# Odd column tiles of a deformable convolution: copied by VectorE and ScalarE in place of DMA transfers, with the pixels of a tile laid column by column

## The chip, the cores and the metric

The kernel runs on one core of one Trainium2 chip, all in 32-bit floats. The metric is the device time of one execution in microseconds (us). The program shown takes 1498.91 us, the median of three runs (1492.4 to 1503.4). The profiled execution is one run of its own, at 1483.92 us.

## The reference, cut to what matters

The input is `x`, 8 images of 128 channels and 64 x 64 pixels. Layer 0 is a group norm and a modulated deformable 3 x 3 convolution, followed by a batch norm over all images and a ReLU. Layer 1 is a group norm and a mixture of four 3 x 3 convolutions and a shared one. The change touches only the deformable convolution:

```python
om = conv(x, off_w) + off_b                      # 27 maps: 9 taps of (dy, dx, mask)
off, mask = om[:, :18], sigmoid(om[:, 18:])
py = dy + row - 1 + ky ; px = dx + column - 1 + kx
val = sum over the four corners of (py, px): weight(corner) * x[corner]   # bilinear
val = val * mask
out = einsum('bckhw,ock->bohw', val, w)
...
x = x + layer0(group_norm(x))
x = x + layer1(group_norm(x))
```

## The kernel before, in words

**Bilinear sampling as a matrix product.** Offsets are taken to be smaller than two pixels (`REACH` 2; if not, a general path runs instead, which these inputs do not take). The samples of a tile of 4 rows by 4 columns (`T` 4) then lie inside a patch of 8 by 8 pixels (`Q` 8, `HALF` 64 pixels). A *band* is two such rows of tiles, `h` = 0 and 1, that is 8 image rows; an image has 8 bands (`NB`), all images 64. A band has 15 column tiles (`NCOL`), which step by 4 columns while a patch is 8 wide, so neighbouring patches overlap by half. The 8 even tiles (`EVEN`) cover the row without overlap; each of the 7 odd tiles consists of the right half of one even patch and the left half of the next.

For every tile a matrix `xts` of 128 partitions by 128 channels holds the pixels: the partition is the pixel of the patch (64 for `h` = 0, then 64 for `h` = 1). Before the change the partition order is `h`, patch row, patch column. The sampling weights are the product of a weight by column, `x_wts`, and one by row, `y_wts`; both have the pixel on the partition.

**The steps of a band `g`:**

- `pick(g)` (L763): VectorE copies the even patches out of the normalised image `pads` into `picked`, two copies of 512 elements.
- `pixels(g)` (L779): TensorE transposes four tiles at a time (L799) into one PSUM tile, ScalarE copies it into `xts` (L802). This is done twice for the even tiles. Only the very first band also makes its odd tiles in this way, from `picked_odd` (L786).
- `share(g)` (L807): fills the odd tiles. For each of the 8 patch columns a transfer takes 16 partitions (one column, all rows, stride 8) of seven even tiles and writes the same partitions of the seven odd tiles. It is issued on SyncE's queue (SP), for one band on GpSimd's (POOL).
- `load_x(g)` (L730) and `load_y(g, k)` (L713): transfers from the tables `x_table` and `y_table` in DRAM into `x_wts` and `y_wts`. A call of `load_y` serves one of the 8 image rows: 5 patch rows (`NR`) by 8 patch columns, 40 partitions, each getting the 9 x 64 floats (`YSTEP`) of its row distance. The parts of `y_wts` out of reach stay zero. In the loop they are issued on POOL, at `q` = 2 and 3.
- `spread(g)` (L746): turns column distances into weights, an Abs on ScalarE with the bias `columns` (L755, L758) and a clip on VectorE (L761).
- `weights(n)` (L822): VectorE multiplies the two weights for one of five groups of three tiles (L837) into `s`, of which there are four buffers; it runs three groups ahead.
- `sample(n)` (L843): TensorE multiplies pixels and weights (L853): 60 matmuls a band, four for each tile, tile after tile from 0 to 14. ScalarE copies the result into `samples` (L863). The PSUM tile `pq` has three buffers.
- `close(g)` (L874) and `conv(g)` (L890): the 3 x 3 convolution of the samples, 9 taps (L902), an eviction by ScalarE (L910) and a store to `ydram` on SP (L912).

**Tables.** `tables(b)` (L308) computes, for an image two ahead, the group norm (means by L317, applied by ScalarE in L342 and VectorE in L346), the offset convolution (combined rows L370, L420, L422; matmuls L389, L455), and from the offsets the tables: gathers through DRAM (`rowwise`, `colwise`, issued on SP in L522, L529, L553, L567), row and column distances on VectorE (L612 to L627), tent functions on ScalarE (L637, L641), masks on VectorE (L674), and the stores `store_x` (L592) and `store_y` (L664). The image itself comes in four quarters by `load_quarter` (L280, SP); `statistics` (L302) reads them.

**What sets the order.** The stage is under a manual schedule: each engine and each queue runs its instructions in the order in which the program issues them. The loop is written by hand (L991): for each band, first the five groups (weights, sample, row-weight loads at `q` 2 and 3), then the taps of the *previous* band's convolution, and between the taps (`part` 0 to 8) everything else: `pixels(g + 2)` at parts 0 and 1, `load_x(g + 3)` at 2, `spread(g + 2)` at 1, 3, 5 and 7, `share(g + 2)` at 3, `pick(g + 3)` and a quarter at 4, and three steps of `tables` after each part (`tick`). `xts` has two buffers, `y_wts` two, `x_wts` three.

Of the kernel before, what the change touches and what calls it, by code (L numbers as in the profile page):

```python
# [11 lines left out]
ALU = mybir.AluOpType  # L12
# [4 lines left out]
P = 128  # L17
H = W = 64
# [21 lines left out]
REACH = 2  # L40
NR = 2 * REACH + 1
T = 4
Q = T + 2 * REACH
HALF = Q * Q
NCOL = 15
NROW = H // T
# [3 lines left out]
EVEN = (NCOL + 1) // 2  # L50
# [5 lines left out]
YSTEP = TAPS * W  # L56
GROW = NR * YSTEP
BLOCK = "block"
OFF_AT = 16
XROW = (NCOL + 1) * T * XSTEP  # L60
# [5 lines left out]
def deform_moe_conv(  # L66
# [18 lines left out]
    nc = tc.nc  # L85
# [10 lines left out]
        out=gsel, in_=gsel, compare_op=ALU.is_ge, fill=0.0, base=0,  # L96
# [3 lines left out]
        out=gsel, in_=gsel, compare_op=ALU.is_ge, fill=0.0, base=3,  # L100
# [49 lines left out]
    def padded(pool, name):  # L150
# [10 lines left out]

    tables_y, tables_x = (
        [dram.tile([n], F32, name=f"tab{a}{i}") for i in range(2)]
        for a, n in (("y", H * GROW), ("x", NROW * XROW))
    )
    y_table, x_table = ([t[b % 2] for b in range(B)] for t in (tables_y, tables_x))

# [12 lines left out]
    def dense():  # L180

        with ExitStack() as st:
# [44 lines left out]

            place_i = a1.tile([P, 3], I32, name="place_i")  # L230
            place = a1.tile([P, 3], F32, name="place")
            beside = a1.tile([P, 1], F32, name="beside")
            for i, base, mask in ((0, T - REACH, T - 1), (1, 0, Q - 1), (2, T, Q - 1)):
                one = place_i[:, i : i + 1]
                nc.gpsimd.iota(one, pattern=[[0, 1]], base=base, channel_multiplier=1)
                nc.vector.tensor_single_scalar(one, one, mask, op=ALU.bitwise_and)
# [5 lines left out]
                    pattern=[[0, 1]], channel_multiplier=sign,  # L242
                )
            nc.vector.tensor_tensor(place[:, 0:1], place[:, 0:1], beside, ALU.add)
            nc.vector.tensor_scalar(place[:, 1:3], place[:, 1:3], -1.0, None, ALU.mult)
            in_tile, columns = place[W:P, 0:1], (place[:, 1:2], place[:, 2:3])

            combos = [a1.tile([P, H // 2, W], F32, name=f"combo{i}") for i in range(2)]
# [19 lines left out]
            xts, ss, late = {}, {}, []  # L268
# [39 lines left out]
            def tables(b):  # L308
# [265 lines left out]
                for k, *where in by_column:  # L574
                    turned_in(nc.sync if b or k == 0 else nc.gpsimd, k, *where)
                if b == 0:
                    share(1, nc.sync)
                yield from pause((50, 9)[b] if b < 2 else 35)

                def moved(side, t, *dims):  # L580
# [81 lines left out]
                def store_y(i, n, rows=slice(0, H)):  # L662

                    nc.sync.dma_start(  # L664
                        out=bass.AP(
                            tensor=y_table[b].tensor,
                            offset=y_table[b].offset + rows.start * GROW + i * YSTEP,
                            ap=[[GROW, rows.stop - rows.start], [1, n * YSTEP]],
                        ),
                        in_=work[rows, i : i + n].rearrange("p i n -> p (i n)"),  # L670
                    )

                def masked(i):
# [27 lines left out]
                for i in (3, 0, 4, 1, 2):  # L701
                    masked(i)
                    store_y(i, 1, soon)
                for k in range(2 * T):
                    load_y(0, k, (nc.sync, nc.gpsimd, nc.scalar, nc.gpsimd)[k % 4])
                for _ in statistics(1):
                    pass
                for tiles in ((NCOL, NCOL + 1), (0, 3), (3, 9), (9, NCOL)):
# [2 lines left out]
                store_x(6, NROW, nc.sync)  # L711
                store_y(0, NR, slice(4 * T, H))

            def load_y(g, k, engine):

                if g >= len(bands):
                    return
                b, j = bands[g]
                h, r = divmod(k, T)
                at = HALF * h + r * Q  # L720
                engine.dma_start(  # L721
                    out=y_wts[g % 2][at : at + NR * Q, r].rearrange("p a b c -> p (a b c)"),
                    in_=bass.AP(
                        tensor=y_table[b].tensor,
                        offset=y_table[b].offset + (2 * T * j + k) * GROW,
                        ap=[[YSTEP, NR], [0, Q], [1, YSTEP]],
                    ),
                )

# [33 lines left out]
            def pick(g):  # L763

                if g >= len(bands):
                    return
                b, j = bands[g]
                for h in range(2):
                    one = pads[b % 2][:, 2 * T * j + T * h : 2 * T * j + T * h + 1, 0:1]
                    nc.vector.tensor_copy(  # L770
                        picked[g % 2][:, :, h],
                        bass.AP(
                            tensor=one.tensor, offset=one.offset,
                            ap=[list(one.ap[0]), [Q, EVEN], [W, Q], [1, Q]],
                        ),
                    )


            def pixels(g, turn_odd=False):  # L779

                if g >= len(bands):
                    return
                xts[g] = a2.tile([P, NCOL, P], F32, name="xt")
                if turn_odd:
                    for side in range(2):
                        nc.vector.tensor_copy(  # L786
                            picked_odd[:, :, :, :, T * side : T * side + T].rearrange(
                                "p c h y x -> p c (h y) x"
                            ),
                            picked[g % 2][  # L790
                                :, 1 - side : EVEN - side, :, :, T * side : T * side + T
                            ].rearrange("p c h y x -> p c (h y) x"),
                        )
                for c0 in range(0, NCOL if turn_odd else EVEN, 4):
                    n = min(4, NCOL - c0)
                    pt = ps_c.tile([P, 4, P], F32, name="pt", tag="pc")
                    for c in range(c0, c0 + n):
                        one = picked[g % 2][:, c] if c < EVEN else picked_odd[:, c - EVEN]
                        nc.tensor.transpose(  # L799
                            pt[:, c - c0], one.rearrange("p h y x -> p (h y x)"), ident  # L800
                        )
                    nc.scalar.copy(xts[g][:, c0 : c0 + n], pt[:, 0:n])  # L802
                    yield

            def share(g, engine):  # L807

                if g >= len(bands):
                    return  # L810
                for x0 in range(T):
                    for side in range(2):
                        rows = slice(x0 + T * side, P, Q)
                        engine.dma_start(  # L814
                            out=xts[g][rows, EVEN:].rearrange("p c n -> p (c n)"),
                            in_=xts[g][rows, 1 - side : EVEN - side].rearrange("p c n -> p (c n)"),
                        )

            def width(q):
                return GT * T + 2 * (q in (0, NGR - 1))  # L820
# [170 lines left out]
            for g in range(len(bands) + 1):  # L991
# [24 lines left out]
                for done, _ in enumerate(taps):  # L1016
                    part, odd = divmod(done, twice)
                    if odd == 0 and part in PIXELS:
                        next(turned, None)
                    if odd == 0 and part == 2:  # L1020
                        load_x(g + 3, nc.gpsimd)
                    if odd == 0 and part in SPREAD:
                        step, half = divmod(SPREAD.index(part), 2)
                        if step:
                            spread(g + 2, HALVES[half], ())
                        else:
                            spread(g + 2, sides_=(half,), clip=False)
                    if odd == 0 and part == 3:
                        share(g + 2, nc.gpsimd if g == 3 else nc.sync)
                    if odd == 0 and j == NB - 3 and part in (0, 1, 2, 4):  # L1030
                        for _ in range(2):
                            next(means_of, None)
                    if odd == 0 and j == NB - 3 and part == 7 and b + 2 < B:
                        for _ in made:
                            pass
                        asked, made = True, tables(b + 2)
                        next(made)
                    if odd == 0 and part in BLOCKS and asked:
                        asked = False
                        tick()  # L1040
                    for _ in range(3 + (g < NB) if twice == 1 else 1 + done % 2):
                        tick()
                    if odd == 0 and part == 4:
                        pick(g + 3)
                        if 2 <= j < 5:
                            load_quarter(b + 2, j - 1)
                    if odd == 0 and part == 8 and j == 1:
                        load_quarter(b + 2, 0)
                for _ in turned:
                    pass  # L1050
                if g == 0:
                    share(2, nc.sync)
                    load_x(3, nc.gpsimd)
                    pick(3)
                    spread(1)
                    for n in range(AHEAD):
                        weights(NGR + n)
                    spread(2)
# [605 lines left out]
```

## Time and profile before

| | us |
|---|---|
| median of three runs | 1498.91 |
| the profiled execution | 1483.92 |
| its span, first to last instruction | 1482.1 |
| the sampling stage, from the first L853 to the last | 71 to 1090 |

| busy in the profiled execution | us | of the span |
|---|---|---|
| TensorE (PE) | 1312.5 | 89% |
| VectorE (DVE) | 961.2 | 65% |
| ScalarE (ACT) | 786.3 | 53% |
| GpSimd (POOL) | 450.7 | 30% |

| instructions that the change touches | count | mean or median each |
|---|---|---|
| `xt<-xt` on SP, L814 | 496 transfers of 56 KB | 587 ns of issue |
| `xt<-xt` on POOL, L814 | 8 transfers of 56 KB | 489 ns of issue, 8.4 us to landing |
| `ywts<-taby` on POOL, L721 | 508 transfers of 90 KB | 611 ns of issue, 5.5 us to landing |
| `picked<-pad`, DVE, L770 | 128 copies of 128x512 | 420 ns |
| `xt<-pt`, ACT, L802 | 130 copies | 584 ns |

Busy shares are averages over the whole span. The row of slices cuts the span in 40 equal parts of 37 us; the sampling stage lies in slices 2 to 29, layer 1 follows. `PEclk` is the TensorE clock granted, in tenths of full speed. In a timeline each line has the start, the length, the engine, the line of the code, the operation, its output and inputs and a count; the bracket gives the idle time before it and the instruction or landing that ended it. `SPq` is SyncE's queue issuing transfers.

### The profile page before, as it was taken

Reading aid. Unit: us, or ns where it says so; the run is one execution under the profiler, and the core shown is the slowest. Engines: PE = TensorE matmul, PEld = TensorE weight load, DVE = VectorE, ACT = ScalarE, POOL = GpSimd, SP = SyncE. Lnnn points to the kernel's source line nnn. Section 1 sums busy time; section 2 is a strip of 40 time slices with the busy share of each in tenths; the row PEclk is TensorE's granted clock in tenths of the full one; section 3 lists DMA queues with packets and bytes.
Section 4 is the critical chain, followed back from the end, with each engine's and each line's share of the span. In section 5 each row is a group of like instructions: output and inputs, shape, how many; then the busy total and the mean of one; then the engine's idle time right before and its main releaser. Section 6 shows DMA issues by size and latency. Waiting matters only on the chain.

```text
span 1482.1 us, 22076 instructions
## 1 busy us (share of the span) xinstructions
PE 1312.5 (89%) x7561; PEld 750.7 (51%) x7561; DVE 961.2 (65%) x1987; ACT 786.3 (53%) x1057; POOL 450.7 (30%) x759
## 2 busy tenths in 40 slices
PE   4169789899998998997999899979985999999997
PEld 1144456565655655664565565656542444444443
DVE  5546666577667755855775685634418887878872
ACT  2355755666675675676567667856624323232320
POOL 6343333343333343343333334344302101011000
PEclk9579979999999998999999899999996999999999
DMA  4496775997798798788869898998908444565411
GB/s 145 116 198 167 168 178 139 199 230 195 183 217 217 170 208 210 190 190 208 194 172 209 208 209 197 206 216 204 219 23 250 133 124 136 147 170 157 113 48 55
DMA packets 136416, 256.27 MB, mean 173 GB/s; under 512 B 81426, under 2 KB 84654, under 8 KB 127606
## 3 DMA queue, kind: packets, MB, share of 16 engines
q0 software_dynamic: 55600, 137.91, 42.9%
q1 hardware_dynamic: 80532, 116.45, 28.1%
q8 instruction: 62, 1.02, 0.3%
q14 instruction: 60, 0.49, 0.1%
q10 hardware_dynamic: 162, 0.41, 0.1%
HBM read 180.23 MB, written 45.35 MB: 152 GB/s over the span
## 4 chain that ended last, share of the span: by engine, by line
PE 44%; DMA 26%; DVE 12%; issue 8%; SPq 5%; ACT 3%; POOL 1%; DVEq 0%; POOLq 0%; ACTq 0%
PE py L902 15%; PE pc L1576 13%; PE pq L853 10%; DMA xt<-xt 10%; DMA pad<-in_x_dram 5%; DMA combo<-rowwise 4%; PE pc L455 2%; DMA yd<-y 2%; PE pt L799 2%; SPq L814 2%; DMA ywts<-taby 2%; SPq L567 2%; DVE combo L422 2%; DMA x<-in_x_dram 1%; DVE s L837 1%
## 5 line engine op out<-in xcount | busy, mean ns | idle before, releaser
L902 PE MATMUL py<-samples,dw_sb 128*128 128x512 f32 (+3 forms) x1296 | 555.9, 564 | 9.5 <-ACT y L910 7.6
L721 POOL DMA_DIRECT2D ywts<-taby x508 | 298.5, 611 | 485.2 <-DVE s L837 381.5
L853 PE MATMUL pq<-s,xt 64*128 64x144 f32 (+1 forms) x3840 | 301.4, 313 | 79.1 <-DVE s L837 48.0
L853 PEld LDWEIGHTS pq<-s,xt 64*128 64x128 f32 x3840 | 272.7, 201 | 124.5 <-issue 45.3
L902 PEld LDWEIGHTS py<-samples,dw_sb 128*128 128x128 f32 x1296 | 229.7, 191 | 208.6 <-issue 178.2
L863 ACT COPY samples<-pq 128x864 f32<-128x864 f32 (+1 forms) x320 | 284.5, 975 | 84.8 <-PE pq L853 84.3
L837 DVE TENSOR_TENSOR s<-xwts,ywts 128x72 f32<-128x72 f32 (+1 forms) x447 | 200.6, 500 | 89.9 <-PE pq L853 76.8
L761 DVE TENSOR_SCALAR xwts<-xwts 128x1152 f32<-128x1152 f32 (+2 forms) x128 | 93.1, 757 | 176.6 <-ACT xwts L755 168.5
L1576 PE MATMUL pc<-v,u 128*128 128x512 f32 x384 | 174.2, 600 | 6.3 <-DVE v L1483 6.3
L1576 PE MATMUL pc<-v,wmix 128*128 128x512 f32 x384 | 174.4, 599 | 0.0
L755 ACT ACTIVATE xwts<-xwts,place 128x1152 f32<-128x1152 f32 (+3 forms) x132 | 152.9, 1162 | 31.3 <-DMA xwts<-tabx 31.3
L1554 ACT ACTIVATE t<-pc,bmix 128x512 f32<-128x512 f32 x32 | 22.0, 687 | 187.5 <-PE pc L1576 98.8
L1576 PEld LDWEIGHTS pc<-v,u 128*128 128x128 f32 x384 | 72.0, 191 | 92.8 <-issue 83.9
L1576 PEld LDWEIGHTS pc<-v,wmix 128*128 128x128 f32 x384 | 72.4, 190 | 91.4 <-issue 89.5
L910 ACT ACTIVATE y<-py,db_sb 128x512 f32<-128x512 f32 (+3 forms) x72 | 45.7, 635 | 130.4 <-PE py L902 88.7
L802 ACT COPY xt<-pt 128x512 f32<-128x512 f32 (+1 forms) x130 | 75.9, 584 | 59.8 <-PE pt L799 55.8
L736 POOL DMA_DIRECT2D xwts<-tabx x128 | 76.3, 608 | 96.1 <-DMA tabx<-combo 33.6
L799 PEld LDWEIGHTS pt<-ident,picked 128*128 128x128 f32 x512 | 59.5, 141 | 75.4 <-ACT xt L802 39.7
L799 PE MATMUL pt<-ident,picked 128*128 128x128 f32 x512 | 79.8, 279 | 5.0 <-ACT xt L802 3.0
L674 DVE TENSOR_TENSOR work<-work,combo 64x576 f32<-64x576 f32 x40 | 29.6, 747 | 46.3 <-ACT work L641 46.3
L982 DVE BATCH_NORM_STATS2 ystats<-y 128x6 f32<-128x512 f32 (+3 forms) x72 | 44.6, 627 | 20.1 <-ACT y L910 20.1
L302 DVE BATCH_NORM_STATS2 stats<-pad 128x6 f32<-128x512 f32 x64 | 39.7, 826 | 14.7 <-DMA pad<-in_x_dram 14.7
(204 smaller groups left out, 1090.6 us busy)
## 6 DMA issues: line engine op xcount, KB each, us to landing
xwts<-tabx POOLq DMA_DIRECT2D x128, 576.0 KB, 8.5
ywts<-taby POOLq DMA_DIRECT2D x508, 90.0 KB, 5.5
xt<-xt SPq DMA_DIRECT2D x496, 56.0 KB
pad<-in_x_dram SPq DMA_DIRECT2D x36, 512.0 KB
out_dram<-yo SPq DMA_DIRECT2D x32, 512.0 KB
yd<-y SPq DMA_DIRECT2D x48, 256.0 KB
pad<-yd SPq DMA_DIRECT2D x16, 512.0 KB
x<-yd SPq DMA_DIRECT2D x16, 512.0 KB
```

The source lines that it names most:

```text
L721: engine.dma_start(out=y_wts[g % 2][at : at + NR * Q, r].rearrange("p a b c -> p (a b c)"), in_=bass.AP(tensor=y_table[b].tensor, offset=y ...
L736: engine.dma_start(out=x_wts[g % 3][HALF * h : HALF * h + HALF], in_=bass.AP(tensor=x_table[b].tensor, offset=x_table[b].offset + (2 * j + ...
L755: nc.scalar.activation(some, some, AF.Abs, bias=columns[side])
L761: nc.vector.tensor_scalar(some, some, -1.0, 0.0, ALU.add, ALU.min)
L799: nc.tensor.transpose(pt[:, c - c0], one.rearrange("p h y x -> p (h y x)"), ident)
L802: nc.scalar.copy(xts[g][:, c0 : c0 + n], pt[:, 0:n])
L837: engine.tensor_tensor(s[:, :, 3 * at : 3 * (at + k)].rearrange("p m (c x) -> p m c x", x=3), by_x[:, :, c : c + k], by_y[:, :, w : w + k] ...
L853: nc.tensor.matmul(by_m[:, h, :, at : at + k], lhsT=xts[g][rows, c // 2 + EVEN * (c % 2)], rhs=s[rows, :, at : at + k], start=True, stop=True,
L863: nc.scalar.copy(bass.AP(tensor=one.tensor, offset=one.offset + first, ap=[list(one.ap[0]), [M * PLANE, 2], [PLANE, M], [WB + 1, 3], [1, w ...
L902: nc.tensor.matmul(py, lhsT=dw_sb[:, 3 * (2 - yy) + 2 - xx], rhs=samples[g % 2][:, m : m + 3 * n - 2 : 3, xx, 1 : W + 1], start=(i == 0), ...
L910: nc.scalar.activation(y, py, AF.Identity, bias=db_sb)
L1576: nc.tensor.matmul(pc, lhsT=us[j][:, kx], rhs=vs[g][:, rows, kx : kx + W], start=(kx == 0), stop=(kx == 2),)
```

## The change

All odd tiles after the first band's are now made by compute engines. The order of the pixels on the partitions becomes `h`, patch column, patch row. The four left and right halves of the patches are then four blocks of 32 partitions that lie together, so `share` becomes four copies of 32 partitions and 896 floats: the two left halves by VectorE, the two right halves by ScalarE, issued at parts 2, 3 (VectorE), 4 and 6 (ScalarE). The new order needs other things: `pick` and the transposes read the patch column first; the biases `columns` are built from another part of the partition number; and the row weights of one patch row now sit 8 partitions apart, so `load_y` serves one of 8 patch rows of both halves (16 partitions) with up to four image rows in one run. For that the y table in DRAM is laid out in runs by patch row: `store_y` writes each row distance `T * YSTEP` floats apart, and the table is longer at its end. At the start, `load_y` of the first band is called once for each half, 16 calls in place of 8.

```diff
-        for a, n in (("y", H * GROW), ("x", NROW * XROW))
+        for a, n in (("y", H * GROW + 4 * NR * YSTEP), ("x", NROW * XROW))
...
-            for i, base, mask in ((0, T - REACH, T - 1), (1, 0, Q - 1), (2, T, Q - 1)):
+            for i, base, mask in ((0, T - REACH, T - 1), (1, 0, HALF - Q), (2, HALF // 2, HALF - Q)):
...
-            nc.vector.tensor_scalar(place[:, 1:3], place[:, 1:3], -1.0, None, ALU.mult)
+            nc.vector.tensor_scalar(place[:, 1:3], place[:, 1:3], -1.0 / Q, None, ALU.mult)
...
-                    share(1, nc.sync)
+                    for piece in range(4):
+                        share(1, piece, MOVES[piece])
...
-                            offset=y_table[b].offset + rows.start * GROW + i * YSTEP,
-                            ap=[[GROW, rows.stop - rows.start], [1, n * YSTEP]],
+                            offset=y_table[b].offset + rows.start * GROW + i * T * YSTEP,
+                            ap=[[GROW, rows.stop - rows.start], [T * YSTEP, n], [1, YSTEP]],
                         ),
-                        in_=work[rows, i : i + n].rearrange("p i n -> p (i n)"),
+                        in_=work[rows, i : i + n],
...
-                for k in range(2 * T):
-                    load_y(0, k, (nc.sync, nc.gpsimd, nc.scalar, nc.gpsimd)[k % 4])
+                for k in range(Q):
+                    for h in range(2):
+                        load_y(0, k, (nc.sync, nc.gpsimd, nc.scalar, nc.gpsimd)[k % 4], (h,))
...
-            def load_y(g, k, engine):
+            def load_y(g, k, engine, halves=(0, 1)):
...
-                h, r = divmod(k, T)
-                at = HALF * h + r * Q
+                first, last = max(0, k - 2 * REACH), min(T - 1, k)
+                n, h = len(halves), halves[0]
                 engine.dma_start(
-                    out=y_wts[g % 2][at : at + NR * Q, r].rearrange("p a b c -> p (a b c)"),
+                    out=y_wts[g % 2][
+                        HALF * h + k : HALF * (h + n) : Q, first : last + 1
+                    ].rearrange("p r a b c -> p (r a b c)"),
                     in_=bass.AP(
                         tensor=y_table[b].tensor,
-                        offset=y_table[b].offset + (2 * T * j + k) * GROW,
-                        ap=[[YSTEP, NR], [0, Q], [1, YSTEP]],
+                        offset=y_table[b].offset
+                        + (2 * j + h) * T * GROW + (T * k + first) * YSTEP,
+                        ap=[[T * GROW, n]] * (n > 1)
+                        + [[0, Q], [1, (last + 1 - first) * YSTEP]],
                     ),
                 )
...
-                            ap=[list(one.ap[0]), [Q, EVEN], [W, Q], [1, Q]],
+                            ap=[list(one.ap[0]), [Q, EVEN], [1, Q], [W, Q]],
...
-            def share(g, engine):
+            def share(g, piece, move):
...
-                for x0 in range(T):
-                    for side in range(2):
-                        rows = slice(x0 + T * side, P, Q)
-                        engine.dma_start(
-                            out=xts[g][rows, EVEN:].rearrange("p c n -> p (c n)"),
-                            in_=xts[g][rows, 1 - side : EVEN - side].rearrange("p c n -> p (c n)"),
-                        )
+                side = piece % 2
+                rows = slice(HALF // 2 * piece, HALF // 2 * (piece + 1))
+                move(
+                    out=xts[g][rows, EVEN:].rearrange("p c n -> p (c n)"),
+                    in_=xts[g][rows, 1 - side : EVEN - side].rearrange("p c n -> p (c n)"),
+                )
+
+            MOVES = (nc.vector.tensor_copy, nc.scalar.copy) * 2
...
-                    if odd == 0 and part == 3:
-                        share(g + 2, nc.gpsimd if g == 3 else nc.sync)
+                    if odd == 0 and part in (2, 3, 4, 6):
+                        piece = {2: 0, 3: 2, 4: 1, 6: 3}[part]
+                        share(g + 2, piece, MOVES[piece])
...
-                    share(2, nc.sync)
+                    for piece in range(4):
+                        share(2, piece, MOVES[piece])
```

Left out are the same change of order, row and column exchanged, in the copies and the transpose of `pixels`.

More of the change, by code (lines that the diff above doesn't have):

```diff
@@ L786, in pixels @@
                         nc.vector.tensor_copy(
-                            picked_odd[:, :, :, :, T * side : T * side + T].rearrange(
-                                "p c h y x -> p c (h y) x"
+                            picked_odd[:, :, :, T * side : T * side + T].rearrange(
+                                "p c h x y -> p c h (x y)"
                             ),
                             picked[g % 2][
-                                :, 1 - side : EVEN - side, :, :, T * side : T * side + T
-                            ].rearrange("p c h y x -> p c (h y) x"),
+                                :, 1 - side : EVEN - side, :, T * side : T * side + T
+                            ].rearrange("p c h x y -> p c h (x y)"),
                         )
@@ L799, in pixels @@
                         nc.tensor.transpose(
-                            pt[:, c - c0], one.rearrange("p h y x -> p (h y x)"), ident
+                            pt[:, c - c0], one.rearrange("p h x y -> p (h x y)"), ident
                         )
```

## The prediction

> **What bounds the kernel now.** I read the page first: busy shares, the row of slices, the chain.
>
> ```profile
> span 1482.1 us, 22076 instructions
> PE 1312.5 (89%) x7561; PEld 750.7 (51%) x7561; DVE 961.2 (65%) x1987; ACT 786.3 (53%) x1057; POOL 450.7 (30%) x759
> ...
> PE   4169789899998998997999899979985999999997
> ...
> PEclk9579979999999998999999899999996999999999
> DMA  4496775997798798788869898998908444565411
> ...
> PE 44%; DMA 26%; DVE 12%; issue 8%; SPq 5%; ACT 3%; POOL 1%; DVEq 0%; POOLq 0%; ACTq 0%
> PE py L902 15%; PE pc L1576 13%; PE pq L853 10%; DMA xt<-xt 10%; DMA pad<-in_x_dram 5%; DMA combo<-rowwise 4%; PE pc L455 2%; DMA yd<-y 2%; PE pt L799 2%; SPq L814 2%; DMA ywts<-taby 2%; SPq L567 2%; DVE combo L422 2%; DMA x<-in_x_dram 1%; DVE s L837 1%
> ```
>
> In slices 2 to 29, the sampling stage that the change touches, TensorE is full except once per batch, where a 7 stands and PEclk dips; DMA is at 7 to 9. The copies `xt<-xt` are 10% of the chain. So the second view is the timeline around one dip.
>
> ```profile
> 676.42 8.23 SPq L814 DMA_DIRECT2D xt<-xt  x8
> ...
> 683.62 0.64 PE L853 MATMUL pq<-s,xt 64*128 64x216 f32 x4
> ...
> 685.84 8.84 SPq L814 DMA_DIRECT2D xt<-xt  x8
> ...
> 691.52 6.04 PE L853 MATMUL pq<-s,xt 64*128 64x144 f32 x56 [7.25 <-DMA yd<-y]
> ...
> 695.04 2.55 SPq L592 DMA_DIRECT2D tabx<-combo  x6
> ...
> 697.70 0.41 SPq L280 DMA_DIRECT2D pad<-in_x_dram  x1
> ...
> 707.25 0.35 PE L317 MATMUL pm<-mv,gsel 128*128 128x1 f32 x2 [1.60 <-DVE mv L305]
> ```
>
> Four of the 60 sampling matmuls are tile 0; the fifth is tile 1, the first odd tile, and there TensorE stands 7.25 us, whatever landing the releaser names. The eight copies hold SyncE for 8 to 9 us of a band that takes 13.2 us undisturbed. The image quarter (L280, 697.70) queues behind them; its statistics then stop TensorE again. The 56 matmuls take 6.04 us where they take 3.83 us undisturbed: the clock has dropped.
>
> Over the stage, waits at the first odd tile are 2.27, 5.73, 0.86, 1.58, 0.73, 2.12, 0.89, 7.25, 6.43 and 0.49: **28 us**. Waits of L317 are 8.25, 5.22, 4.39, 1.60 and 0.40: **20 us**. Sampling and mean matmuls stretched after those waits lose about **17 us** (1.67, 2.06, 1.66, 2.21 and 2.80 in the 56-matmul groups, the rest after L317).
>
> The third view is ScalarE, in a plain band and then in one that builds tables.
>
> ```profile
> 652.07 1.12 ACT L755 ACTIVATE xwts<-xwts,place 128x1008 f32<-128x1008 f32 x1
> 656.31 0.69 ACT L910 ACTIVATE y<-py,db_sb 128x512 f32<-128x512 f32 x1 [3.12 <-issue]
> ```
>
> ```profile
> 430.02 0.69 ACT L641 ACTIVATE work<-work 64x576 f32<-64x576 f32 x1
> 430.62 0.66 ACT L910 ACTIVATE y<-py,db_sb 128x512 f32<-128x512 f32 x1
> ```
>
> The plain band leaves 3.1 us ahead of the eviction, the table band nothing. VectorE is the same in the band of the combos (columns: window and length, then busy us of PE, PEld, DVE, ACT, POOL, clock, DMA share, GB/s):
>
> ```profile
> 600.00:613.00 13.00, 12.90 (x104) 6.71 (x102) 12.83 (x16) 6.66 (x10) 3.05 (x6) 1.00 0.73 191
> ```
>
> [...] copies of 512 and 768 elements take 420 and 559 ns, 0.54 ns an element over 142 ns. [...] the trace's 64x576 Relu (L641) takes 682 ns [...].
>
> **The change, part by part.**
>
> *Removed:* 504 transfers of 56 KB (496 on SP, 8 on POOL), 28 MB of 256 MB. Everything behind them on SP moves up: image quarters, table stores, evictions to `yd`, offset gathers. The first-odd-tile waits go. Of the L317 waits I keep a fifth, since the 10.7 us that SP spends on five column gathers (664.61) also delays quarters. Gain 28 + 16 + 17 = **61 us**. What is late next: the copies' own engines.
>
> *VectorE copies:* two per band, 7x128 = 896 elements: 142 + 896 x 0.54 = 0.63 us, 1.25 us a band. Queued behind the first are the clips (L761), table work and `pick`, whose next readers are the weights and TensorE. It waits for the second ScalarE copy L802, about 2 us after the weights end; in plain bands VectorE idles 4.5 us there, so nothing. In the combo band it is full (L837 already holds TensorE 0.36 us): full price.
>
> *pick:* same elements, inner read stride 256 B. No such read is in the trace; the nearest, the copy L519 that writes at 64 B stride, took 602 ns against 420. Bounds 420 [...] and about 690 ([...] L616, 804 ns for 576, suggests a little over). I take 600: 0.36 us a band, hidden except in the combo band. Together 1.6 us once for each of six batches' tables (2 to 7): **10 us**.
>
> *ScalarE copies:* [...] 1.9 us a band. Behind them stand the eviction of `py` and the next band's sample copies, which run back to back (4.4 us) into the transposes; a late start reaches TensorE almost whole. Plain bands: 3.1 us free, cost nothing; without that cover, 1.9 us each. Table bands: at 404-418 a 1.28 us idle before L659 takes part, leaving 0.8; at 418-431 no room, 1.6; the next 0.25; the affine band (590.08, L342 four times 0.8 us) 2.3, as its slow clock goes too. Sum 5 us by six: **30 us**.
>
> *y table:* the store's runs shrink from 11.5 KB to 2.3 KB, same bytes, seven whole stores and one split, SP now less loaded: 0, bounds -2 to +5. The load keeps eight transfers on POOL and 720 KB. [...] They are issued third to fifth, 1.8 us or more after the start at 658.38; the reader comes at 673.74, 15.4 us later. So 0 to 1 us a band; I take 0.
>
> *Start:* 16 half loads instead of 8 (POOL four more of 0.6 us), copies for bands 1 and 2: between -2 and +5, I take +1. `place`, the transposes and `picked_odd` (389 ns, once) keep their sizes: 0.
>
> Sum: 10 + 30 + 1 - 61 = **-20 us**. The profiled execution took 1483.9 us (span 1482.1), so 1464 on its own scale; the median shown, 1498.9, is 1% above it, and the same difference gives **1479 us**.
>
> **The rivals.**
>
> *Copies find room everywhere* (chance 0.20). For it: ScalarE is 53% busy, VectorE 65%, and waits inside table bands can shift. Against: the two full bands above. Half of the 40 us loss gone, and SP's relief whole: about -45, 1454 us.
>
> *Slower: ScalarE becomes the bound in table bands* (0.20). Four of them pay 1.9 us whole and the combo band 1.6 plus 1.75 for the late copy L802: 11 us a batch; three stalls over 2 us then halve the clock, at 1.7 us each: 16 x 6 = 96, less 61: +35, 1534 us. It decides from 10 us a batch. For it: no idle ahead of 430.62. Against: 7.25 us stalls vanish, and small ones, such as 1.58, kept the clock.
>
> *The y loads become a wait* (0.11): 1 us a band for 60 bands, less 20: +40, 1539 us. [...]
>
> *The transfers were hidden anyway* (0.07): another landing, of offsets or quarters, ends last; gains shrink to the losses, 1499 us. Against: the stop after exactly four matmuls.
>
> **How the numbers follow.** My forecast has 0.42, its own range 1462 to 1498. About 1% can be told from no change: 15 us, so faster means below 1484. Forecast: 0.27 faster, 0.15 same. Adding the rivals: faster 0.27 + 0.20 = 0.47; same 0.15 + 0.07 + 0.01 = 0.23; slower 0.20 + 0.10 = 0.30. The range 1440 to 1530 takes in most of the first rival and the lesser half of both slower ones; about 0.2 stays out.
>
> **What would show it.** Right: no stop after four sampling matmuls, SP with no `xt<-xt`, L317 waits under 2 us, copies near 0.63 and 0.93 us, `pick` near 600 ns, TensorE waits of 1 to 2 us before L799 and L853 in table bands. Wrong: a landing of `ywts` over 12 us with VectorE waiting on it; ScalarE late in plain bands; PEclk dips as many as now.

## The result, and the profile after

The changed kernel takes **1473.27 us** (median of four runs, 1468.3 to 1475.7), against 1495.66 us for the kernel before on the same chip (four runs, 1489.7 to 1503.4). The ratio is **0.986, 95% interval 0.982 to 0.990**: 1.4% faster, where 1479 was forecast. The profiled executions are 1472.76 after (1464 was forecast on that scale) and 1483.92 before; the latter lies 12 us under its median, so profile differences are smaller than those of the medians. One execution of the experiments below, 1471.84 us with `pick` in its old order, was slow for its kernel and is left out of the median given there.

The lines of the page of after that answer to those shown of before: span, busy shares, the slices of TensorE's clock and of the transfers, and the shares of the chain.

```profile
span 1471.0 us, 21219 instructions
PE 1300.3 (88%) x7561; PEld 740.1 (50%) x7561; DVE 1064.9 (72%) x2113; ACT 902.7 (61%) x1183; POOL 448.5 (30%) x755
...
PEclk9579989999999999999999999999997999999999
DMA  4485755976887598598778778777618544565411
...
PE 46%; DMA 16%; DVE 15%; issue 10%; ACT 9%; POOL 3%; SPq 1%; DVEq 0%; ACTq 0%; POOLq 0%
```

`xt<-xt` has left the chain, where it had 10%, and transfers fall from 26% to 16% of it. In the sampling stage the clock row is flat after its first slices; before, it showed two more dips, to 8. Now subtract TensorE's busy time from the span: 1482.1 - 1312.5 = 169.6 us before, 1471.0 - 1300.3 = **170.7 us** after. TensorE stands still just as long as before. The gain of the profiled run is shorter matmuls: with a mean granted clock of 0.960 in place of 0.946 they fill 12.2 us less. So the stops were exchanged, not removed. Where they went is seen by asking what TensorE waited for in the window from 230 to 960 us (columns: who waits, for what; us in total, times, longest). Before:

```profile
PE pq L853 <- DMA xt<-xt: 11.7, 5, 6.4
PE pm L317 <- DVE mv L305: 11.6, 4, 5.2
PE pq L853 <- DMA pad<-in_x_dram: 7.8, 2, 5.7
PE pq L853 <- DMA yd<-y: 7.3, 1, 7.3
```

After:

```profile
PE pq L862 <- ACT samples L872: 29.6, 16, 5.8
PE pq L862 <- DVE s L846: 6.2, 6, 1.8
...
PE pm L318 <- DVE mv L306: 3.8, 4, 1.1
```

The landings are gone and TensorE's waits for means (L318) are 1.1 us at most. In their place TensorE waits for ScalarE, which evicts the samples late (L872), and for weights. Within a band, no stop after four sampling matmuls is left; the stops now come after 36, at the fourth of the five groups, which needs one of the three `pq` buffers evicted.

That looks like the forecast's own reason, ScalarE's copies. One such stop, with ScalarE ahead of it, says something else:

```profile
671.89 2.73 PE L862 MATMUL pq<-s,xt 64*128 64x144 f32 x24 [3.85 <-ACT samples L872]
```

```profile
659.41 0.59 ACT L810 COPY xt<-pt 128x512 f32<-128x512 f32 x1 [0.74 <-PE pt L807]
663.26 1.25 ACT L763 ACTIVATE xwts<-xwts,place 128x1152 f32<-128x1152 f32 x1 [3.26 <-DMA xwts<-tabx]
...
665.87 1.89 ACT L821 COPY xt<-xt 32x896 f32<-32x896 f32 x2
...
670.26 0.67 ACT L919 ACTIVATE y<-py,db_sb 128x512 f32<-128x512 f32 x1
670.83 3.39 ACT L872 COPY samples<-pq 128x1008 f32<-128x1008 f32 x4
```

ScalarE's two copies take 1.89 us ahead of the late eviction, but ScalarE had stood 3.26 us before that for x rows that had not landed. Either could be the cause.

### The profile page after: what moved, and what is told of

It is laid out like the page before. It is cut to its first block, busy times and chain, and to the rows that moved or that the text cites. A ratio compares the mean times of both kernels' runs of the same rounds, so it can differ in the third digit from the quotient of the medians.

```text
span 1471.0 us, 21219 instructions
## 1 busy us (share of the span) xinstructions
PE 1300.3 (88%) x7561; PEld 740.1 (50%) x7561; DVE 1064.9 (72%) x2113; ACT 902.7 (61%) x1183; POOL 448.5 (30%) x755
## 4 chain that ended last, share of the span: by engine, by line
PE 46%; DMA 16%; DVE 15%; issue 10%; ACT 9%; POOL 3%; SPq 1%; DVEq 0%; ACTq 0%; POOLq 0%
PE py L911 16%; PE pc L1587 14%; PE pq L862 10%; DMA ywts<-taby 5%; DMA xwts<-tabx 4%; DVE s L846 3%; PE pt L807 2%; PE pc L456 2%; DVE combo L423 2%; ACT xwts L763 2%; DVE stats L303 2%; POOL ywts L725 2%; DVE xwts L769 2%; DVE combo L421 1%; DMA pad<-in_x_dram 1%
## 5 line engine op out<-in xcount | busy, mean ns | idle before, releaser
L862 PE MATMUL pq<-s,xt 64*128 64x144 f32 (+1 forms) x3840 | 294.1, 307 | 90.8 <-DVE s L846 50.6
L862 PEld LDWEIGHTS pq<-s,xt 64*128 64x128 f32 x3840 | 264.5, 195 | 136.0 <-ACT samples L872 55.3
L872 ACT COPY samples<-pq 128x864 f32<-128x864 f32 (+1 forms) x320 | 282.5, 972 | 53.0 <-PE pq L862 52.1
L846 DVE TENSOR_TENSOR s<-xwts,ywts 128x72 f32<-128x72 f32 (+1 forms) x447 | 199.5, 500 | 68.6 <-PE pq L862 59.2
L763 ACT ACTIVATE xwts<-xwts,place 128x1152 f32<-128x1152 f32 (+3 forms) x132 | 153.0, 1163 | 23.4 <-DMA xwts<-tabx 21.5
L821 DVE COPY xt<-xt 32x896 f32<-32x896 f32 x126 | 78.5, 623 | 114.2 <-ACT xt L810 113.2
L769 DVE TENSOR_SCALAR xwts<-xwts 128x1152 f32<-128x1152 f32 (+2 forms) x128 | 92.9, 755 | 39.9 <-ACT xwts L763 26.3
L821 ACT COPY xt<-xt 32x896 f32<-32x896 f32 x126 | 118.0, 936 | 2.4
L778 DVE COPY picked<-pad 128x512 f32<-128x512 f32 x128 | 72.1, 605 | 1.5 <-PE pt L807 0.8
```

The source lines that it names most:

```text
L763: nc.scalar.activation(some, some, AF.Abs, bias=columns[side])
L769: nc.vector.tensor_scalar(some, some, -1.0, 0.0, ALU.add, ALU.min)
L821: move(out=xts[g][rows, EVEN:].rearrange("p c n -> p (c n)"), in_=xts[g][rows, 1 - side : EVEN - side].rearrange("p c n -> p (c n)"),)
L846: engine.tensor_tensor(s[:, :, 3 * at : 3 * (at + k)].rearrange("p m (c x) -> p m c x", x=3), by_x[:, :, c : c + k], by_y[:, :, w : w + k] ...
L862: nc.tensor.matmul(by_m[:, h, :, at : at + k], lhsT=xts[g][rows, c // 2 + EVEN * (c % 2)], rhs=s[rows, :, at : at + k], start=True, stop=True,
L872: nc.scalar.copy(bass.AP(tensor=one.tensor, offset=one.offset + first, ap=[list(one.ap[0]), [M * PLANE, 2], [PLANE, M], [WB + 1, 3], [1, w ...
```

## The experiments

Theory 1 is the prediction's sum: the stops and the clock are worth 61 us, the copies cost about 40, three quarters of it on ScalarE. Its rivals are told in the expectations. Runs of the kernel before on the same chip gave 1494 to 1501 us, so compare by ratios; all times are medians.

**The new layout with transfers in place of copies.** The four pieces are issued as transfers of 112 KB at part 3, once from SP (the diff), once from GpSimd (`nc.gpsimd.dma_start` in its place).

```diff
-            MOVES = (nc.vector.tensor_copy, nc.scalar.copy) * 2
+            MOVES = (nc.sync.dma_start,) * 4
...
-                    if odd == 0 and part in (2, 3, 4, 6):
-                        piece = {2: 0, 3: 2, 4: 1, 6: 3}[part]
-                        share(g + 2, piece, MOVES[piece])
+                    if odd == 0 and part == 3:
+                        for piece in range(4):
+                            share(g + 2, piece, MOVES[piece])
```

> The changed kernel with its new pixel order and y table, but the odd tiles filled by four transfers of 112 KB on SyncE's queue again (no engine copies). Queue theory (the gain came from clearing SyncE's queue, the loss is the copies' engine time): the waits at the first odd tile and the late image quarters come back in part, since four issues take about half the queue time of eight, and the 40 us of engine time are gone: 1470 to 1490 us. Traffic theory (the gain came from 28 MB less for the DMA engines): as before, 1490 to 1500. Table theory (the y table in runs did it): as the changed kernel, 1473.

> The same four transfers, but issued on GpSimd's queue, so SyncE's queue is as free as in the changed kernel while the bytes are moved as before. Queue theory: quarters are early, no L318 wait over 2 us, no engine time: 1450 to 1475 us, if the transfers land in time behind the x loads. Traffic theory: 1490 to 1500.

Measured: 1508.92 on SP (ratio 1.009, 1.006 to 1.013) and 1500.47 on GpSimd (1.004, 1.001 to 1.008). SP now issues a band's transfers in 2.4 to 5.4 us (median 2.8 in the window), where eight took 4.9 to 11.8 (median 5.6), and TensorE hardly waits at an odd tile (on SP three times, 1.6 us together in the window). The time came back elsewhere: ScalarE stood 71.0 us (SP) and 67.2 us (GpSimd) for x rows, against 31.3 in the kernel before and 21.5 in the changed one (over the whole span), and on SP four waits for means cost 21.8 us. Against the same layout without any copies (1465, below), four transfers cost 44 us on SP and 36 on GpSimd, where the eight of the kernel before cost 78 in the old layout: they are 34 to 42 us cheaper, which is no more than what the new layout turns out to cost below. The queue theory's times failed in both runs, though its mark on GpSimd held (waits for means of 1.2 us at most); the traffic theory's 1490 to 1500 us are met by GpSimd's run at their edge and not by SP's. So how much of the old transfers' cost lay in SyncE's queue and how much in their bytes stays open.

**One engine for all four pieces.** Same places, all by VectorE; then by ScalarE; then VectorE in the first seven bands of an image and ScalarE in the last (where a list by `j` takes the place of `MOVES[piece]`). The diff is the first kernel's; the second has `nc.scalar.copy`.

```diff
-            MOVES = (nc.vector.tensor_copy, nc.scalar.copy) * 2
+            MOVES = (nc.vector.tensor_copy,) * 4
```

> The changed kernel with all four copies on VectorE. If ScalarE's two copies cost 30 us in table bands, as predicted: ScalarE waits before sampling (about 36 us in all) mostly go, VectorE pays 1.25 us more in each of six combo bands (8 us): 1445 to 1460 us. If ScalarE is late there for another reason (late x or gather landings): 1470 to 1480.

> All four pieces copied by ScalarE at the same places, none by VectorE. Theory 1: ScalarE, already late in four bands of eight, gets 1.87 us more a band: 30 us or more on top of 1473, 1500 to 1520. Theory 2: VectorE's 1.25 us a band leave the path, ScalarE's lie beside it: 1440 to 1465. The run in which VectorE had all four pieces took 1534, 61 us over the changed kernel.

> The changed kernel with all four copies on VectorE in bands 0 to 6 of an image and on ScalarE in band 7, where VectorE is full with the combined rows. If engine time in full bands is what the copies cost: 5 to 12 us under all_on_vector, 1438 to 1455 us. If not: equal to all_on_vector.

Measured: 1533.56 (1.024, 1.021 to 1.028), 1529.19 (1.023, 1.016 to 1.030) and 1506.41 (1.009, 1.005 to 1.013). VectorE had no room for them: the times forecast for the first and third kernel, below the changed one's, failed. Still, giving ScalarE the copies of one band in eight took 27 us off VectorE's kernel, where 5 to 12 were expected. ScalarE's kernel came out 9 us beyond theory 1's range, and theory 2 failed. TensorE's waits in the same window, for VectorE's kernel and then for ScalarE's:

```profile
PE pq L862 <- DVE s L846: 37.4, 12, 7.7
PE pq L862 <- ACT samples L872: 20.3, 9, 5.0
```

```profile
PE pq L862 <- ACT samples L872: 54.5, 22, 5.0
```

Each engine, given all four, makes its own wait grow: L846 from 6.2 to 37.4 us, L872 from 29.6 to 54.5. The distance between the first sampling matmuls of successive bands shows where. With VectorE's two further copies, the bands without table work stay as they are (13.1, 13.1 and 12.2 us, now 13.1, 13.2 and 12.2); the five with it go, in the batch from 639 us (678 us here), from 18.9, 17.9, 13.1, 17.2 and 21.0 to 19.7, 21.6, 14.8, 16.9 and 25.0 us. The second and the last grow by 3.7 and 4.0 us for two more copies of 0.62 each. Waits are half of the loss: the clock falls to 0.939 and 0.942, and matmuls fill 1332 and 1325 us in place of 1300.

**No copies at all, and one engine's alone.** The odd columns are sampled from the even tiles, so nobody reads the odd ones; the copies are then left out, or one engine's are still issued.

```diff
-                            lhsT=xts[g][rows, c // 2 + EVEN * (c % 2)],
+                            lhsT=xts[g][rows, c // 2 + EVEN * (c % 2) * (g < 3)],
...
-                    if odd == 0 and part in (2, 3, 4, 6):
+                    if g < 1 and odd == 0 and part in (2, 3, 4, 6):
```

With one engine's copies kept, the last line admits parts 2 and 3 (VectorE) or 4 and 6 (ScalarE).

> From the fourth band on no odd tile is copied: the odd columns are sampled from the even tiles, so that part of the computation is left out; the new layout of pick, y table and loads stays. Theory 1 (the prediction's sum): the copies cost 30 us on ScalarE and 7.5 us on VectorE, so 1473 - 37 = about 1436. Theory 2 (VectorE is on the path in all table bands, and ScalarE's lateness is handed on from it): copies cost 40 to 60 us, nearly all VectorE's, 1415 to 1433. Theory 3 (the waits of TensorE in the changed kernel come from late loads, not from copies): 1460 or more.

> Odd columns sampled from the even tiles from the fourth band on; VectorE's two copies a band are still issued at their places, ScalarE's two are left out. Theory 1: ScalarE's 30 us come back, 1443. Theory 2: little comes back, 1460 to 1470. Theory 3: 1465 or more.

> Odd columns sampled from the even tiles from the fourth band on; ScalarE's two copies a band are still issued at their places, VectorE's two are left out. Theory 1: VectorE's 7.5 us come back, 1466. Theory 2: most comes back, 1425 to 1445. Theory 3: 1465 or more.

Measured: 1464.54 (0.981, 0.974 to 0.989), 1479.84 (0.986, 0.979 to 0.993) and 1469.52 (0.982, 0.977 to 0.987). Leaving all copies out brings **about 9 us, not 37**; by the intervals, between nothing and some 20. Theories 1 and 2 fall; the times of all three are theory 3's. VectorE's copies alone even took 7 us more than both engines' together, with overlapping intervals. The sums of TensorE's waits in the window order the engines better than the times do: 35.5 us with no copies, 36.2 with ScalarE's, 49.4 with VectorE's, 47.6 with both. ScalarE's copies cost almost nothing. Their cover is a wait: over the whole span ScalarE stands for x rows (L763)

```profile
ACT xwts L763 <- DMA xwts<-tabx: 49.0, 18, 7.5
```

with no copies, and only 21.5 us in the changed kernel, where the copies fill that time. So the late x rows are what stays when the copies go. The copies don't make the rows late: they land in 9.4 us with them and in 9.5 without.

ScalarE's copies leave two marks. The same stretch of the eighth band of an image, without copies and with ScalarE's alone:

```profile
709.42 4.28 PE L862 MATMUL pq<-s,xt 64*128 64x216 f32 x60
```

```profile
704.81 2.60 PE L862 MATMUL pq<-s,xt 64*128 64x216 f32 x36
708.26 1.93 PE L862 MATMUL pq<-s,xt 64*128 64x144 f32 x24 [0.85 <-ACT samples L872]
```

This stop of 0.9 us comes in five of the eight images. In the sixth band the stop after 36 matmuls rises from 1.0 to 1.5 us, as it does with VectorE's copies alone. In the fifth it doesn't rise: 2.1 to 5.0 us without copies, 0.8 to 2.4 with ScalarE's (four images, the third to the sixth).

**The kernel before without its transfers.** The same edit in `before`, old layout and old loads.

> The kernel before, old layout and old loads, with the eight odd-tile transfers a band left out from the fourth band on; the odd columns are sampled from the even tiles, so that part of the computation is left out. Theory 1 (the prediction's gain of 61 us: the stops and the clock come back in full): 1496 - 61 = about 1435. Theory 4 (behind the odd-tile stops stand waits for the table chain and for x loads, which come out when the stops go; the kernel without copies in the new layout took 1465): 1455 to 1470, with TensorE waiting in the same bands for samples evicted late or for weights instead. If it is below 1450 the new layout itself costs 15 us or more.

Measured: **1422.52 us**, ratio 0.948 (0.943 to 0.954): 78 us under the kernel before by the medians, and 42 us (49 by the ratios) under the kernel without copies, which does the same work in the new layout. Theory 4 fails; so does theory 1's 1435, on the low side. The last line of the expectation is what held: the layout itself costs. The two pages beside each other, first this kernel, then the one without copies (page: span, packets, the queue of GpSimd's transfers; then KB of a transfer and us to landing):

```profile
span 1423.6 us, 21100 instructions
...
q0 software_dynamic: 55344, 137.45, 42.9%
...
xwts<-tabx POOLq DMA_DIRECT2D x128, 576.0 KB, 7.9
ywts<-taby POOLq DMA_DIRECT2D x508, 90.0 KB, 4.8
```

```profile
span 1457.5 us, 21087 instructions
...
q0 software_dynamic: 79472, 137.50, 44.9%
...
xwts<-tabx POOLq DMA_DIRECT2D x128, 576.0 KB, 9.5
...
ywts<-taby POOLq DMA_DIRECT2D x126, 144.0 KB, 7.9
```

The queue moves the same 137.5 MB, in 24,128 more packets; its only transfers of another form are the y loads. They land in 7.0 to 7.9 us by size where they took 4.8, and the x loads on the same queue, themselves unchanged, in 9.5 in place of 7.9.

**Pick or loads?** The new layout differs by `pick` too (605 against 420 ns). So the kernel without copies once more, with the old reading order; a tile's pixels then stand in the order that the weights don't match.

```diff
-                            ap=[list(one.ap[0]), [Q, EVEN], [1, Q], [W, Q]],
+                            ap=[list(one.ap[0]), [Q, EVEN], [W, Q], [1, Q]],
```

> The kernel without copies in the new layout (1465), with one more edit: VectorE's pick reads the pixels in the order of the kernel before, so that one takes 420 and not 605 ns; the pixels of a tile then stand in the old order, which the weights don't match, so that part of the computation is changed. Between the kernel without copies (1465) and the kernel before without transfers (1423) lie 42 us for the new layout. Theory 5 (the y loads in runs by row make the x rows land late: 9.5 against 7.9 us, ScalarE waits 56 against 17 us for them): the 0.37 us a band of pick are a small part, 1450 to 1462, and ScalarE's wait for x rows stays at 45 us or more. Theory 6 (VectorE is on the path in every table band, pick's 0.37 us a band count in full with what hangs on them): 1425 to 1445, and that wait falls below 30 us.

Measured: 1454.86 (0.976, 0.971 to 0.981), 10 us under the kernel without copies, with overlapping intervals; `pick` took 418 ns. Of the new layout's cost some 10 us are `pick`'s and **some 32 the y table's and the loads'** (8 and 41 by the ratios, 12 and 22 by the profiled executions); from here to the old layout the intervals are apart. The time is theory 5's, and its second mark is just met: the 56 us that it starts from are ScalarE's waits at L763 for any landing (49.0 put down to x rows, 7.2 to y rows), and the same sum is 45.0 here (34.8 and 10.2) and 17.0 in the old layout. X rows still land in 9.5 us.

**The x loads ahead of the y loads.** If late x rows make the waits, moving only them must help the changed kernel itself.

```diff
+                        if q == 2 and g and j != NB - 3:
+                            load_x(g + 3, nc.gpsimd)
                         if q in (2, 3):
                             for k in range(T * (q - 2), T * (q - 1)):
...
-                    if odd == 0 and part == 2:
+                    if odd == 0 and part == 2 and j == NB - 3:
                         load_x(g + 3, nc.gpsimd)
```

> The changed kernel; only the two x loads of each band move on GpSimd's queue, from behind that band's y loads and the second tap to ahead of the y loads at the third group of columns. Theory 4 (in the band where tables start, ScalarE waits 3.3 us for x rows that land late, and TensorE then 3.9 us for samples): the x rows come some 3 us or more earlier, the wait before ScalarE's first absolute value there is below 1 us, and the time falls by 5 to 20 us, 1453 to 1468. Theory 1 (ScalarE's copies make those waits): no difference, 1470 to 1476. If the y loads then come late instead: VectorE waits for y rows, 1475 to 1490.

Measured: **1458.72 us**, ratio 0.974 (0.968 to 0.980), below the changed kernel's interval and the shortest of the kernels that leave nothing out. Theory 4 holds. The same stop as above, in this kernel, ScalarE and then TensorE:

```profile
654.17 0.58 ACT L810 COPY xt<-pt 128x512 f32<-128x512 f32 x1 [0.74 <-PE pt L807]
654.66 1.26 ACT L763 ACTIVATE xwts<-xwts,place 128x1152 f32<-128x1152 f32 x1
```

```profile
663.32 1.92 PE L862 MATMUL pq<-s,xt 64*128 64x144 f32 x24 [0.51 <-ACT samples L872]
```

ScalarE doesn't stand at L763, and TensorE's stop shrinks from 3.85 to 0.51 us with the two copies still in the chain between them. Over the whole span ScalarE's waits for x rows at L763 fall from 21.5 to 4.4 us, and the rows land in 7.8 us in place of 9.4. The stop in the fifth band, where most of the new layout's cost sits (2.1 to 5.0 us without copies, at most 2.0 in the old layout without transfers), shrinks to between 0.5 and 1.3 us; the 0.9 us in the eighth band, which only ScalarE's copies make, stay. The price appears where the expectation's last sentence looked for it, without the loss named there: VectorE now waits 39.8 us for y rows at its weights, 1.5 before, while TensorE's waits for weights rise only from 6.2 to 8.2 us in the window.

**GpSimd's own engine.**

```diff
-            MOVES = (nc.vector.tensor_copy, nc.scalar.copy) * 2
+            MOVES = (nc.gpsimd.tensor_copy,) * 4
```

> All four pieces copied by GpSimd's own compute engine at the same places, none by VectorE or ScalarE. GpSimd is 30 per cent busy, but issues the x and y loads[...]. Theory 4: with copies of 1 to 2 us each, 4 to 8 us a band lie ahead of the x loads, which land later: 1475 to 1510. Theory 1: ScalarE's and VectorE's terms go, 1436 to 1450.

Measured: 1530.48 (1.023, 1.017 to 1.029), beyond both ranges. A copy takes 1182 ns, so 4.7 us a band, and x rows land in 9.8 us. That alone doesn't explain it: TensorE's waits move to VectorE (L846: 51.6 us in the window), whose own instructions became longer. The clip (L769) in the changed kernel, then in this one (busy us, mean ns, idle before):

```profile
L769 DVE TENSOR_SCALAR xwts<-xwts 128x1152 f32<-128x1152 f32 (+2 forms) x128 | 92.9, 755 | 39.9 <-ACT xwts L763 26.3 <-DMA ywts<-taby 8.1 <-ACT xwts L766 4.3
```

```profile
L769 DVE TENSOR_SCALAR xwts<-xwts 128x1152 f32<-128x1152 f32 (+2 forms) x128 | 115.8, 934 | 167.6 <-ACT xwts L763 143.8 <-DMA ywts<-taby 20.0 <-ACT xwts L766 3.8
```

The product rises from 500 to 557 ns, `pick` from 605 to 711. These means mix two kinds. Here are two clips with no GpSimd copy beside them, then two with one:

```profile
655.53 1.42 DVE L769 TENSOR_SCALAR xwts<-xwts 128x1152 f32<-128x1152 f32 x2
...
667.00 4.70 POOL L821 COPY xt<-xt 32x896 f32<-32x896 f32 x4
668.37 2.54 DVE L769 TENSOR_SCALAR xwts<-xwts 128x1152 f32<-128x1152 f32 x2 [3.73 <-ACT xwts L763]
```

Of the 122 clips of this form 70 overlap no GpSimd copy and take 754 ns, as in the changed kernel; the 52 that overlap one take 1196. For `pick` it is 603 and 1078 ns, for the product of 432 elements 607 and 1094, but for the statistics of L991 684 and 682. Why the first three took longer beside a copy and the statistics didn't, no run shows.

## Why the prediction was right, and where not

The time was right, and the mechanism of the gain; the account of the loss was not, and that the sum came out is luck. The table sets its sum beside the runs, read from the profiled spans, from the medians and from the ratios (as us of 1496). For the new layout with the old `pick` the profiled execution is the fastest of that kernel's, so its column puts the y loads low and `pick` high.

| step | predicted | by the profiles | by the medians | by the ratios |
|---|---|---|---|---|
| transfers, their stops and the clock (before → before without transfers) | -61 | 1482.1 → 1423.6: -58.5 | 1500.8 → 1422.5: -78 | -77 |
| y table and loads (→ new layout, old pick, no copies) | 0 | → 1445.9: +22.3 | → 1454.9: +32 | +41 |
| `pick` (→ new layout, no copies) | 2 | → 1457.5: +11.6 | → 1464.5: +10 | +8 |
| copies (→ the changed kernel) | 38 | → 1471.0: +13.5 | → 1473.3: +9 | +7 |

Predicted for `pick` is 0.36 us in six combo bands, for the copies the rest of the 10 us plus ScalarE's 30; 1 us for the start stands apart.

- **The gain of 61: right by the profiles that it was read from, and there in its parts.** From before to before without transfers TensorE's busy time falls by 1312.5 - 1296.3 = 16.2 us, where 17 were given for the clock, and its idle time by 169.6 - 127.3 = 42.3 us, where 44 were given for the stops. The medians say 78, in the main because the profiled execution of before was 17 us under the median of that comparison. Two readings were loose: in slices 2 to 29 the row of TensorE has three 7s, not one a batch, and the clock dips in other slices than these; and the 8 to 9 us for which eight copies held SyncE are those of the bands around the dip, in most other bands it was 5 to 6.
- **The unit prices: right.** 0.63 and 0.93 us for the copies and 600 ns for `pick` were forecast; 623, 936 and 605 ns were measured. The 0.93 us was the author's estimate; the trace of before has ScalarE's copies of 864 and 1008 floats (L863) at 923 and 1051 ns.

```profile
L821 DVE COPY xt<-xt 32x896 f32<-32x896 f32 x126 | 78.5, 623 | 114.2 <-ACT xt L810 113.2
...
L821 ACT COPY xt<-xt 32x896 f32<-32x896 f32 x126 | 118.0, 936 | 2.4
...
L778 DVE COPY picked<-pad 128x512 f32<-128x512 f32 x128 | 72.1, 605 | 1.5 <-PE pt L807 0.8
```

- **Plain bands cost nothing: right.** They kept 13.1 and 13.2 us even with four copies on VectorE; with four on ScalarE one of them grew to 14.0.
- **The step that failed: "Sum 5 us by six: 30 us" for ScalarE.** Its copies alone measure 5 us by the medians and nothing by the profiles (1456.8 against 1457.5). Where the forecast put 0.8, 1.6, 0.25 and 2.3 us a batch, TensorE's stops in the fifth to the eighth band, where a late start would arrive, grew by nothing, 0.5, nothing and 0.9 us. The first term is covered by a wait: in the band at 404 to 418, where the trace of before left 1.28 us, ScalarE waits for x rows in the new layout, and the copies fill such waits (49.0 us without them, 21.5 with). With all four pieces on ScalarE the margin is used up and the time rises by 56 us; so the rival "ScalarE becomes the bound" named a real limit, at twice the load.
- **VectorE: "Together 1.6 us once for each of six batches' tables" was too small, by an amount that isn't clear of the noise.** By the sums of waits VectorE's copies cost 11 to 14 us (47.6 - 36.2 and 49.4 - 35.5), by the medians 4 and 15, and `pick` some 10. The forecast counted one full band a batch. In the changed kernel VectorE is busy for 17.46 of 17.88 us in the sixth band and for 17.01 of 17.21 us in the eighth, that of the combos (batch from 639 us).
- **The other failed term: "So 0 to 1 us a band; I take 0" for the y loads.** The bound was right, and 22 to 41 us over 60 bands, 0.4 to 0.7 us each, lie inside it; the value taken was not. The argument compared the landing of the largest y loads with VectorE's reader of y and found 15.4 us of room. How late they would land was the author's estimate, shown by no trace; in the changed kernel the y loads landed in 6.7 to 7.9 us by size (medians), 5.5 before. That reader indeed hardly waits (1.5 us at the weights in the changed kernel). The price fell on a neighbour: the x loads behind the y loads on GpSimd's queue (without copies 9.5 us to landing, 7.9 in the old layout), and ScalarE that reads them. Why the new form lands later wasn't isolated: 24,128 more packets came with it, and no run here separates them from the rest of the form.

The forecast's total is therefore right by an exchange of errors: by the ratios 31 us too much on the copies and a gain 16 us larger than forecast, against 41 us missing for the loads and 6 for `pick`. What all copies cost once the x rows come in time stays open: the kernel with the x loads first was not run without copies.

## What to carry to other kernels

When a long stop goes, subtract busy time from the span before and after: if the difference stays, the stop was exchanged, and only leaving the new work out says what it costs. When a transfer changes form, look past its own reader to the transfers behind it on the queue and to who waits for those. Work split over two engines can fit into slack that neither has for all of it: here two pieces each cost about 9 us together, and four on either engine over 60.

## What the runs showed of the hardware

- Beside GpSimd copies of 32x896 floats (1182 ns) some VectorE instructions took longer: the clip 1196 in place of 754 ns, `pick` 1078 in place of 603; the statistics of L991 took 682 beside one and 684 without.
- A copy that reads SBUF at a stride of 256 bytes took 605 ns, with 420 for the same 512 elements in the old order.
- Stops came with a lower clock: in the kernel with all copies on VectorE, TensorE's idle time grew, against the changed kernel, by 202.3 - 170.7 = 31.6 us and its busy time for the same matmuls by 32.0 us, at a granted clock of 0.939 in place of 0.960.
- In the kernel before, a stop of TensorE of 2.12 us (ended at 558.17) was followed by 3.41 us at half the granted clock; after one of 1.58 us (ended at 432.56) the clock stayed full.
- Two loads on one queue: with the y loads in their new form, the unchanged x loads behind them landed in 9.5 us in place of 7.9; moved ahead of them, in 7.8.
